# A second layer-1 bank, more of its bias on ScalarE, node copies on GpSimd and an earlier first quad, in a graph network on one core

## The chip, the cores and the metric

The kernel runs on one core of one Trainium2 chip. The metric is the device time of one execution in microseconds. Each kernel was run four times or more, on the same chip beside the kernel before; the experiments were spread over two chips, and the medians of the kernel before lie between 595.3 and 596.6 us in all rounds.

Names used below: PE is TensorE, PEld its weight loads, DVE is VectorE, ACT is ScalarE, POOL is GpSimd. A *ten* is ten chunks in a row, the period in which the kernel's plan repeats. A *turn* is a transpose by PE; its result lies in a bank until ACT or DVE has read it. For the masks of the edges, DVE's *threshold* marks the node i of each edge (`tp`), a *node copy* widens these marks from fp16 to fp32r (`i`), and a *mark product* of PE multiplies them with the *positions* (`posall`, made by POOL) to find the node j. The *bias table* is `b1t`. The *root* is the square root of the layer-0 variance (`m_sd`); `sh` holds it split into a rounded part and a rest, and making the rest is a small step of POOL. In the update network, `ysum` are the summed messages, and `uh` and `uy` the two hidden layers.

## The reference

Each of 128 graphs has 64 nodes with 128 features. For every pair (i, j) with an edge, a small network gives a message; the messages of a node are summed, and a second network updates the node.

```python
def _mlp(x, w0, b0, g0, be0, w1, b1, g1, be1, w2, b2):
    h = relu(x @ w0 + b0)
    h = layernorm(h, g0, be0)
    h = relu(h @ w1 + b1)
    h = layernorm(h, g1, be1)
    return h @ w2 + b2

messages = _mlp(concat(f_i, f_j), msg...) * adjacency[..., None]
agg      = sum(messages, axis=2)
updated  = x + _mlp(concat(x, agg), upd...)
```

All is float32. Some 13.5% of the pairs are edges (the kernel has room for 640 edges in each graph, and a slow path if that is exceeded, which does not run here: the fullest graph has 622).

## The kernel before

Edges are packed into tiles of 128. A chunk is four tiles and fills one of the kernel's banks (128x512 f32 in the trace); there are 160 chunks. Five chunks are a *quad* of graphs and share one table of statistics. The normalisation of layer 0 is folded into layer 1: with a weight matrix whose columns are centred, the layer-1 sum is `h @ w1c + sd * b1b`, where `sd` is a number for each edge, the root of the layer-0 variance. So the "bias" of layer 1 is different for each edge. It can be made in two ways: by a matmul (a table `b1t` against the turned roots `sdT`), or by ACT, which writes `b1b` scaled by `sd` into the bank ahead of the products, four instructions of 128 columns for a chunk. The second is called a *seed*.

```python
ps_k, ps_h, ps_t, ps_z, ps_y = ...           # one bank each
ps_a = ...tile_pool(name="ps_a", bufs=2, space=PSUM)   # turns
ps_u = ...                                   # update layers

def node_rows(p):                            # node marks of a pair of graphs, fp16 -> fp32r
    IR[p] = tpp.tile([P, CAP], F32R, name="i32", bufs=2)
    nc.scalar.copy(IR[p], TP[p])             # then a DMA puts it into the tile s

def layer0(n):                               # two matmuls a piece into hps, then
    ...
    nc.scalar.activation(H[n], ps, AF.Relu, bias=b0c)

def stats0(n):                               # PE turns h into the bank hT, DVE takes statistics
    ...
def seed(n):
    q, c = divmod(n, QC)
    Z[n] = zbank().rearrange("p (t c) -> p t c", t=CH)
    for t in range(CH):
        nc.scalar.activation(Z[n][:, t, :], W["b1b"], AF.Copy, scale=SR[q][:, k:k + 1])

def layer1(n):
    if n in Z:
        ps = Z.pop(n)                        # seeded
    else:
        ps = (hbank if n >= NCHK - L1 and n % 2 else zbank)()
        nc.tensor.matmul(ps, lhsT=SD[q], rhs=W["b1t"][...], start=True, stop=False, ...)
    for t in range(CH):
        nc.tensor.matmul(ps[:, t, :], lhsT=h[:, t * P:(t + 1) * P], rhs=W["w1c"], ...)
    nc.scalar.activation(Y[n], ps, AF.Relu)

for n in range(1, NCHK - L1 - 1):            # NCHK = 160, L1 = 8, CPB = 10
    if n % CPB in (0, 1, 6, 9):
        at(n + L1 - 1, "b", seed, n)
...
for n in range(last + 1):                    # the plan; every engine keeps this order
    run(n, "a"); run(n, "m")                 # "a": ACT's copies out of banks
    layer1(n - L1)
    run(n, "b")
    layer0(n)
    stats0(n - 1)
    run(n, "k")
    stats1(n - L1)
    for k in ("x", "x1", "x2", "e0", "e1", "e"):
        run(n, k)                            # "x": PE's turns and update layers
```

(cut: the making of the edge masks, the update network, the slow path, and the launch)

Eight PSUM banks hold all this: mk, hps, hT, z, ys, two for turns, one for the update layers. That an engine keeps one order shows in the traces: from 180 to 480 us the sequence of ACT's instructions repeats without an exception with every ten, 67 of them.

## Time and profile before

| | before |
|---|---|
| time, median of all runs beside the changed kernel | 595.59 us (594.19 to 598.19) |
| first layer-1 ReLU begins | 40.1 us |
| next 30 chunks | 100.3 us |
| a ten in the middle (chunks 30 to 140) | 33.88 us |
| chunks 140 to 150 | 33.2 us |
| from there to the end | 47.5 us |

The start of the ReLU that ACT makes of each layer-1 bank is a clean mark, once a chunk; the distances between the marks tell where time goes. The lines of the page and of the windows view that matter are shown in the prediction. In a line of groups, the first pair of numbers is busy time and the mean of one, and what follows is the idle time ahead of them with its releaser. PE's busy time is made of modelled ends of matmuls; this turns out to matter (300 ns between two starts where 28 ns is the shortest, below).

### The profile page before, as it was taken

What the parts mean: (1) busy time and instruction counts of PE and PEld (TensorE: products, weight loads), DVE (VectorE), ACT (ScalarE), POOL (GpSimd) and SP (SyncE); (2) the same over time, 40 slices, a digit from 0 to 9 for tenths busy, and PEclk for the clock granted to TensorE, in tenths of its full rate; (3) what the DMA queues carried; (4) which work ended last, traced back from release to release, by engine and by line L of the source; (5) the groups of instructions that cost most, each with busy time, mean ns of one, the idle gap of its engine ahead of it and who ended that gap; (6) DMA issues with size and microseconds to landing.
All of it is one profiled execution on the core that took longest, in us unless ns stands there. A gap on an engine that the chain in (4) does not pass through costs nothing. (4 is left out here: it accounts for less than half of the span.)

```text
span 593.9 us, 15761 instructions
## 1 busy us (share of the span) xinstructions
PE 565.6 (95%) x5333; PEld 521.2 (88%) x5333; DVE 480.6 (81%) x1944; ACT 479.3 (81%) x1087; POOL 296.5 (50%) x840
## 2 busy tenths in 40 slices
PE   7778899999999999999999999999999999999894
PEld 4667789899999999999999999999999999999883
DVE  4568778697988979797987979798897979788576
ACT  5677878888888888888898888888898888887434
POOL 2443435454655546365654545365654636446352
PEclk7599999999999999999999999999999999999999
DMA  4354544566454544645355445545554385531201
GB/s 98 90 120 99 134 104 109 96 121 126 114 124 109 127 106 102 147 114 131 85 140 122 98 116 120 131 114 133 97 127 110 93 143 112 107 96 37 47 19 40
DMA packets 90769, 63.22 MB, mean 106 GB/s; under 512 B 57398, under 2 KB 74812, under 8 KB 90684
## 3 DMA queue, kind: packets, MB, share of 16 engines
q1 hardware_dynamic: 90396, 62.03, 46.7%
q8 instruction: 44, 0.72, 0.6%
q14 instruction: 41, 0.34, 0.2%
q10 hardware_dynamic: 288, 0.13, 0.1%
HBM read 6.82 MB, written 4.19 MB: 19 GB/s over the span
## 5 line engine op out<-in xcount | busy, mean ns | idle before, releaser
L546 DVE BATCH_NORM_STATS2 st<-hT 128x6 f32<-128x128 f32 x640 | 141.3, 283 | 51.7 <-PE hT L542 51.7
L595 PE MATMUL z<-w1c,h 128*128 128x128 f32 x1248 | 168.3, 278 | 2.4 <-ACT z L581 2.3
L595 PEld LDWEIGHTS z<-w1c,h 128*128 128x128 f32 x1248 | 159.1, 191 | 12.6 <-issue 5.0
L605 DVE BATCH_NORM_STATS2 st<-y 128x6 f32<-128x128 f32 x640 | 137.7, 278 | 2.7 <-ACT y L598 1.4
L249 POOL TENSOR_TENSOR m_d<-st 128x20 f32<-128x20 f32 x62 | 17.1, 276 | 208.8 <-DVE st L546 188.8
L598 ACT ACTIVATE y<-z 128x512 f32<-128x512 f32 x156 | 93.5, 600 | 29.7 <-PE z L595 26.6
L536 ACT ACTIVATE h<-hps,b0c 128x512 f32<-128x512 f32 x160 | 109.1, 682 | 4.9 <-PE hps L533 4.9
L542 PE MATMUL hT<-ident,h 128*128 128x128 f32 x640 | 98.0, 276 | 2.1 <-DVE st L546 2.1
L661 POOL TENSOR_TENSOR w<-oh,m_q 128x320 f32<-128x320 f16 x126 | 91.3, 741 | 10.2 <-PE hT L542 5.6
L581 ACT ACTIVATE z<-b1b,m_sd 128x128 f32<-128x128 f32 x240 | 89.1, 371 | 7.3
L533 PE MATMUL hps<-s,abl 128*128 128x512 f32 (+3 forms) x256 | 92.7, 374 | 1.9 <-ACT h L536 1.1
L542 PEld LDWEIGHTS hT<-ident,h 128*128 128x128 f32 x640 | 76.8, 142 | 12.4 <-DVE st L546 1.4
L533 PE MATMUL hps<-s,abh 128*128 128x512 f32 (+3 forms) x256 | 79.0, 327 | 0.0
L674 PE MATMUL ys<-y,w 128*64 128x128 f32 x1280 | 76.9, 275 | 0.0
L674 PEld LDWEIGHTS ys<-y,w 128*64 128x64 f32 x1280 | 69.2, 137 | 7.0 <-issue 6.6
L515 DVE TENSOR_TENSOR j<-mk,cmpt 128x320 fp32r<-128x320 f32 x124 | 58.8, 474 | 0.5 <-PE mk L507 0.5
L479 ACT ACTIVATE d<-slot,mid 128x640 f16<-128x640 f16 x64 | 53.7, 840 | 0.0
L533 PEld LDWEIGHTS hps<-s,abl 128*128 128x128 f32 x256 | 49.8, 194 | 4.0 <-ACT h L536 2.1
L533 PEld LDWEIGHTS hps<-s,abh 128*128 128x128 f32 x256 | 49.9, 195 | 0.0
L464 ACT CAST abh<-mu 128x512 fp32r<-128x512 f32 (+1 forms) x33 | 18.9, 573 | 36.9 <-PE mu L452 36.9
L592 PE MATMUL z<-b1t,sdT 80*128 80x512 f32 x96 | 47.2, 491 | 0.6 <-ACT y L598 0.2
L491 ACT CAST i<-tp 128x640 fp32r<-128x640 f16 x62 | 44.8, 722 | 2.2 <-DVE tp L485 2.2
(218 smaller groups left out, 1005.5 us busy)
## 6 DMA issues: line engine op xcount, KB each, us to landing
s<-i SPq DMA_DIRECT2D x124, 160.0 KB, 2.7
s<-j SPq DMA_DIRECT2D x124, 160.0 KB, 2.7
xn<-in_x_dram SPq DMA_DIRECT2D x15, 256.0 KB, 3.7
out_dram<-uo SPq DMA_DIRECT2D x15, 256.0 KB, 2.4
an<-in_adj_dram SPq DMA_DIRECT2D x16, 128.0 KB, 2.6
oh<-tp SPq DMA_TRANSPOSE x64, 2.7
xn<-in_x_dram SPq DMA_DIRECT2D x2, 128.0 KB
out_dram<-uo SPq DMA_DIRECT2D x2, 128.0 KB, 2.3
```

Of the source, the lines that this page charges most:

```text
L479: nc.scalar.activation(D[p], slot, AF.Abs, bias=blocks[b]["mid"][:, q:q + 1], scale=-1.0)
L515: nc.vector.tensor_tensor(JR[p][:, c], MK.pop((p, k))[:, 0:HC], cmpt[:, c], op=ALU.is_equal)
L533: nc.tensor.matmul(ps[:, c:c + w], lhsT=ab[:, g % 4, :], rhs=s, start=(k == 0), stop=(k == 1))
L536: nc.scalar.activation(H[n], ps, AF.Relu, bias=b0c)
L542: nc.tensor.transpose(ps[:, t, :], H[n][:, t * P:(t + 1) * P], ident)
L546: nc.vector.bn_stats(ST0[q][:, CH * c + t, :], ps[:, t, :])
L581: nc.scalar.activation(Z[n][:, t, :], W["b1b"], AF.Copy, scale=SR[q][:, k:k + 1])
L595: nc.tensor.matmul(ps[:, t, :], lhsT=h[:, t * P:(t + 1) * P], rhs=W["w1c"], start=False, stop=True, skip_group_check=True)
L598: nc.scalar.activation(Y[n], ps, AF.Relu)
L605: nc.vector.bn_stats(ST1[q][:, CH * c + t, :], Y[n][:, t, :])
L661: (nc.vector if p == NP - 2 else nc.gpsimd).tensor_tensor(WT[p][:, :, g, :], OH[p][:, :, g * N:(g + 1) * N], Q[q][:, k:k + TG].unsqueeze(2 ...
L674: nc.tensor.matmul(YS[b][g * N:(g + 1) * N, k, :], lhsT=w[:, t, g, :], rhs=y, start=(t == 0), stop=(t == TG - 1))
```

## The change

The intent: PE is full, so take bias matmuls from it by seeding seven chunks of ten, not four. ACT then needs room: the node copies go to GpSimd. The seeds need time: layer 1 gets two banks by parity, so that a seed is written two chunks ahead; its bank is taken from the turns, whose plan is spread out. And at the start the first quad's layer-0 chunks are made before the masks of later pairs.

```diff
-        ps_z = ...tile_pool(name="ps_z", bufs=1, space=PSUM)
+        ps_z = [...tile_pool(name=f"ps_z{k}", bufs=1, space=PSUM) for k in range(2)]
-        ps_a = ...tile_pool(name="ps_a", bufs=2, space=PSUM)
+        ps_a = ...tile_pool(name="ps_a", bufs=1, space=PSUM)
...
-            nc.scalar.copy(IR[p], TP[p])
+            nc.gpsimd.tensor_copy(IR[p], TP[p])
...
+        def z_of(n):
+            if n not in Z:
+                Z[n] = zbank(n % 2).rearrange("p (t c) -> p t c", t=CH)
+            return Z[n]
...
-        for n in range(1, NCHK - L1 - 1):
-            if n % CPB in (0, 1, 6, 9):
-                at(n + L1 - 1, "b", seed, n)
+        for n in range(2, NCHK - L1):
+            if n % CPB in (0, 1, 2, 4, 6, 7, 9):
+                at(n + L1 - 2, "x", seed, n)
...
+        LEAD = 3
-        STEADY = (1, 2, 3, 3, 4, 7, 8, 6, 8, 9, 12, 13, 11, 14, 15)
+        STEADY = (1, 1, 2, 3, 4, 7, 8, 6, 8, 9, 12, 13, 11, 14, 15)
...
-            n = q * QC + QC
+            n = q * QC + QC if q else LEAD
...
-            if 1 < n < NCHK:
-                layer0(n)
-            if 1 <= n - 1 < NCHK - 1:
-                stats0(n - 1)
+            if n + LEAD < QC or QC <= n < NCHK:
+                layer0(n if n >= QC else n + LEAD)
+            if n + 1 < QC or QC <= n - 1 < NCHK - 1:
+                stats0(n - 1 if n > QC else n + 1)
```

(cut: the order of the first masks before the loop, the banks of the last update units, and the places of the count and of the first turn of features)

More of the change, by code (lines that the diff above doesn't have):

```diff
@@ L302, in edge_path @@
         ps_t = es.enter_context(tc.tile_pool(name="ps_t", bufs=1, space=PSUM))
-        ps_z = es.enter_context(tc.tile_pool(name="ps_z", bufs=1, space=PSUM))
+        ps_z = [es.enter_context(tc.tile_pool(name=f"ps_z{k}", bufs=1, space=PSUM)) for k in range(2)]
         ps_y = es.enter_context(tc.tile_pool(name="ps_y", bufs=1, space=PSUM))
-        ps_a = es.enter_context(tc.tile_pool(name="ps_a", bufs=2, space=PSUM))
+        ps_a = es.enter_context(tc.tile_pool(name="ps_a", bufs=1, space=PSUM))
         ps_u = es.enter_context(tc.tile_pool(name="ps_u", bufs=1, space=PSUM))
@@ L317, in hbank, with tbank, zbank @@
             return ps_h.tile([P, CH * P], F32, name="hps")
-        def zbank():
-            return ps_z.tile([P, CH, C], F32, name="z").rearrange("p t c -> p (t c)")
+        def tbank():
+            return ps_t.tile([P, CH, P], F32, name="hT").rearrange("p t c -> p (t c)")
+        def zbank(k):
+            return ps_z[k].tile([P, CH * C], F32, name=f"z{k}")
         plan = {}
@@ L430, in odd_weights, with turn_x @@
                                     axis=AX.X, op=ALU.max, apply_absolute_value=True)
-        def turn_x(b, q0=0, q1=PB):
+        def turn_x(b, q0=0, q1=PB, bank=abank):
             blk = blocks[b]
-            ps = blk["x_ps"] = abank()
+            ps = blk["x_ps"] = bank()
             for q in range(q0, q1):
@@ L572, in root_out @@
             SD[q] = t
+        SEEDED = set()
+        def z_of(n):
+            if n not in Z:
+                Z[n] = zbank(n % 2).rearrange("p (t c) -> p t c", t=CH)
+            return Z[n]
         def seed(n):
             q, c = divmod(n, QC)
-            Z[n] = zbank().rearrange("p (t c) -> p t c", t=CH)
+            z_of(n)
+            SEEDED.add(n)
             for t in range(CH):
@@ L585, in layer1 @@
             q, c = divmod(n, QC)
+            ps = z_of(n)
+            del Z[n]
             h = H.pop(n)
-            if n in Z:
-                ps = Z.pop(n)
-            else:
-                ps = (hbank if n >= NCHK - L1 and n % 2 else zbank)()
-                ps = ps.rearrange("p (t c) -> p t c", t=CH)
+            if n not in SEEDED:
                 nc.tensor.matmul(ps, lhsT=SD[q], rhs=W["b1t"][:, CH * c:CH * c + CH, :],
@@ L681, in edge_path, with __init__ @@
         class Unit:
-            def __init__(self, b, k0, n, eng, bank):
-                self.b, self.k0, self.n, self.eng, self.bank = b, k0, n, eng, bank
+            def __init__(self, b, k0, n, eng, bank, turns=abank):
+                self.b, self.k0, self.n, self.eng, self.bank, self.turns = b, k0, n, eng, bank, turns
                 self.s = slice(k0 * P, (k0 + n) * P)
@@ L716, in turn @@
         def turn(u, src):
-            u.ps = abank()
+            u.ps = u.turns()
             for q in range(u.n):
@@ L794, in edge_path @@
             if b > 0:
-                r = max(o - 13, 1)
+                r = max(o - 12, 1)
                 at(max(o - 14, 0), "m", rank, b)
@@ L819, in edge_path @@
             else:
-                units = [(Unit(b, 2, 2, nc.vector, zbank), NCHK + L1 + 1, LAST[3], 1, 1),
-                         (Unit(b, 0, 2, nc.gpsimd, hbank), NCHK + L1 - 1, LAST[2], 3, 3)]
+                units = [(Unit(b, 2, 2, nc.vector, lambda: zbank(1), tbank), NCHK + L1 + 1, LAST[3], 1, 1),
+                         (Unit(b, 0, 2, nc.gpsimd, lambda: zbank(0), hbank), NCHK + L1 - 1, LAST[2], 3, 3)]
             for u, n, t, m0_at, xo_at in units:
@@ L850, in edge_path @@
             if p > 1:
-                at(max(n - 7, p - 2), "a", distance, p)
-                at(max(n - 6, p - 2), "m", make_tp, p)
-                at(max(n - 5, 1), "a", node_rows, p)
-                at(max(n - 4, 1), "a", stack, p, 0, IR)
+                if p > 2:
+                    at(max(n - 7, p - 2), "a", distance, p)
+                    at(max(n - 6, p - 2), "m", make_tp, p)
+                at(n - 5, "a", node_rows, p)
+                at(n - 4, "a", stack, p, 0, IR)
                 for k in range(2):
@@ L867, in edge_path @@
         for q in range(NQ):
-            n = q * QC + QC
+            n = q * QC + QC if q else LEAD
             last = q == NQ - 1
+            end = q * QC + QC + L1
             at(n, "e0", var0_of, q)
@@ L873, in edge_path @@
             at(n + 2, "x" if last else "a", root_out, q)
-            at(n + L1 - last, "e1", var1_step, q)
+            at(end - last, "e1", var1_step, q)
             wait = 0 if last else 1 if q == NQ - 2 else 2
-            at(n + L1 + wait, "a", root1_of, q)
-            at(n + L1 + wait, "m", inverse_of, q)
-        for n in range(1, NCHK - L1 - 1):
-            if n % CPB in (0, 1, 6, 9):
-                at(n + L1 - 1, "b", seed, n)
+            at(end + wait, "a", root1_of, q)
+            at(end + wait, "m", inverse_of, q)
+        for n in range(2, NCHK - L1):
+            if n % CPB in (0, 1, 2, 4, 6, 7, 9):
+                at(n + L1 - 2, "x", seed, n)
         warm = ubank()
@@ L895, in edge_path @@
         count_out(0)
-        turn_x(0, 0, 2)
+        turn_x(0, 0, 2, tbank)
         turn_x_out(0, 0, 2)
@@ L910, in marks_here, with rows_here @@
             marks(p, 0)
-            marks(p, 1, zbank)
+            marks(p, 1, lambda: zbank(p % 2))
+        def rows_here(p, g):
+            nc.scalar.copy(S[p][0:N, g, :], TP[p][g * N:(g + 1) * N])
         def compare_here(p, g):
             s = slice(g * N, (g + 1) * N)
-            nc.scalar.copy(S[p][0:N, g, :], TP[p][s])
             for k in range(2):
@@ L919, in compare_here @@
                                         op=ALU.is_equal)
+            if g:
+                MK.pop((p, 0)), MK.pop((p, 1))
         marks_here(0)
         rows(0, 0, 2, 4)
+        rows_here(0, 0)
+        rows_here(0, 1)
         compare_here(0, 0)
@@ L927, in edge_path @@
         compare_here(0, 1)
-        MK.pop((0, 0)), MK.pop((0, 1))
         make_tp(1)
+        distance(2)
+        marks_here(1)
         layer0(1)
         rows_hi(0, 0, 2, 4)
-        marks_here(1)
+        rows_here(1, 0)
+        rows_here(1, 1)
         compare_here(1, 0)
         rows_lo(0, 0, 2, 4)
+        layer0(2)
+        make_tp(2)
+        compare_here(1, 1)
+        nc.vector.memset(ones_row, 1.0)
         stats0(0)
-        compare_here(1, 1)
-        MK.pop((1, 0)), MK.pop((1, 1))
-        nc.vector.memset(ones_row, 1.0)
         at(0, "x", turn_x, 0, 2, PB)
```

## The prediction

> **What bounds the kernel now.** The graphs are worked off as 160 chunks of four edge tiles. In iteration n TensorE (PE) does layer 1 of chunk n-8 (bias and product into the bank z), layer 0 of chunk n (bank hps), the turns of chunk n-1 (bank hT), and then smaller work. ScalarE (ACT) empties z and hps with ReLUs, VectorE (DVE) takes the statistics, and every engine keeps program order. I read the page first, its busy shares and its slices:
>
> ```profile
> PE 565.6 (95%) x5333; PEld 521.2 (88%) x5333; DVE 480.6 (81%) x1944; ACT 479.3 (81%) x1087; POOL 296.5 (50%) x840
> ...
> PE   7778899999999999999999999999999999999894
> ...
> PEclk7599999999999999999999999999999999999999
> ```
>
> PE is filled from about the sixth slice (75 us) on; before that it is not, and its clock is low in the first two slices. The windows view, 100 us at a time, gives the middle:
>
> ```profile
> 200.00:300.00 100.00, 99.92 (x979) 93.62 (x978) 85.36 (x348) 87.41 (x199) 53.78 (x153) 1.00 0.50 117
> 300.00:400.00 100.00, 99.91 (x980) 93.71 (x979) 85.64 (x349) 87.24 (x198) 54.61 (x156) 1.00 0.49 117
> 400.00:500.00 100.00, 99.91 (x981) 93.84 (x980) 85.58 (x349) 87.21 (x199) 54.61 (x156) 1.00 0.54 115
> ```
>
> The columns after the length are PE, weight loads, DVE, ACT, POOL (GpSimd). PE is busy 99.9 of 100 us at full clock. As ends of matmuls are modelled, I checked with starts: the ReLUs of layer 1 begin 33.9 us apart from one ten of chunks to the next, and the distances from each matmul's start to the next one's add up to the same with no hole in them. So in the middle PE alone sets the pace, and a microsecond counts there only if PE's work shrinks. The groups by line name the parts that the change touches:
>
> ```profile
> L592 PE MATMUL z<-b1t,sdT 80*128 80x512 f32 x96 | 47.2, 491 | 0.6 <-ACT y L598 0.2
> ...
> L581 ACT ACTIVATE z<-b1b,m_sd 128x128 f32<-128x128 f32 x240 | 89.1, 371 | 7.3
> ...
> L491 ACT CAST i<-tp 128x640 fp32r<-128x640 f16 x62 | 44.8, 722 | 2.2 <-DVE tp L485 2.2
> ```
>
> L592 is the bias of layer 1 as a matmul (100 in the program); L581 is the same bias written by ACT, four instructions a chunk, for 60 of 160 chunks; L491 is the node copy, 62 times. Last, the waits of PE:
>
> ```profile
> PE ma L566 <- POOL sh L561: 4.4, 4, 2.0
> PE mk L507 <- DVE tp L485: 4.4, 2, 3.2
> PE z L595 <- ACT z L581: 2.3, 4, 0.9
> ```
>
> These few (total, times, longest) all lie before 110 us. That is the start, where PE is not yet the bound.
>
> [...] the threshold L485, 0.37 us in the median, took 1.23 us when it began at 29.18 us together with a POOL product of 1.04 us; no other after 10 us is long.
>
> **The change, part by part.**
>
> *Bias matmuls.* Counting the conditions, seeds rise from 60 chunks to 105 (seven of ten, chunks 2 to 151), so bias matmuls fall from 100 to 55: 45 fewer. The page's 491 ns is not their price, as neighbours overlap. By starts in the middle, L592 begins 28 ns after the matmul before it where that is a turn of the root, and the product begins 336 ns after L592; without L592 the product begins 109 ns after such a turn. Net 28 + 336 - 109 = 255 ns; where a mark product precedes, 28 + 336 - 136 = 228. I take 250 ns. 45 x 0.25 = 11.3 us, 0.75 us of each ten chunks, nearly all on the path: PE's ten chunks go from 33.9 to about 33.1 us.
>
> *ACT.* ACT's records overlap too, so I use starts: a seed of four takes 4 x 0.38 = 1.52 us, a copy 0.615. Ten chunks gain three seeds (+4.6) and lose four copies (-2.5): +2.1. All ACT instructions of ten chunks add up to 28.8 us this way (85% of 33.9), afterwards 30.9 (93% of 33.1). Still under PE, but no longer far.
>
> *Two banks.* The seed was written between the ReLU of chunk n-1 and PE's need of z for chunk n, with one bank. Now it is written two iterations ahead, into the bank that chunk n-2 has left, after the ReLU that empties hps. PE's waits for seeds (2.3 us and as much again of weight loads, partly the same time) should go: 2 us, early.
>
> *One bank less for turns.* ps_a falls from two buffers to one. The order of the program shows how they made room: before, features and counts, and the turns of ysum and uy, fell into the same iteration; after, every user has its own, and ACT empties each at the head of the next. I charge 0 to 1 us.
>
> *Node copies on POOL.* No copy is in the trace there. POOL's iota of 640 elements took 0.66 us, its 512-wide residual sum with two inputs 1.28 us; I estimate 0.8 us, so 62 x 0.8 = 50 us, and POOL goes from 54% to some 65% in the middle. A copy has an iteration or more before its DMA is due, so this lies beside PE's work. What it can cost is DVE waits of the kind seen at 29 us.
>
> *Start.* The first ReLU of layer 1 begins at 40.1 us. From 9 to 40 us PE is busy 22.6 us by the windows view and idle 8.4, of it 3.2 for the threshold that DVE reaches late and 2.0 for the roots (L566). With three layer-0 chunks ahead and the first statistics done two iterations earlier, these two waits are attacked; the total work up to there is the same, and it runs partly at low clock. I estimate 2 to 3 us. *End:* other banks, same order: 0.
>
> Sum: -11.3 (bias matmuls) -2 (seed waits) -2.5 (start) +2 to 3 (new waits) = about -13.
>
> **Rivals.**
>
> *ACT becomes the bound in places.* For: iterations are unequal. Over four light ones (layer 1 of chunks 81 to 84) PE has 1.9 + 2.5 + 3.4 + 2.0 = 9.7 us afterwards and ACT 2.3 + 3.3 + 2.3 + 3.3 = 11.2, a lag of 1.5 us; before it was 10.2 against 9.4, with a lag of 1.0 at most after the first. PE needs hps emptied each iteration. Against: a seed now stands behind the ReLU that PE waits for, so that much lag can be borne, and an iteration of 5.4 us on PE follows in which ACT catches up. If 0.5 us of each ten chunks is lost, 7 us go and the result is near 589 us.
>
> *POOL blocks or delays.* [...] Against: a copy starts as its threshold ends[...]; only in the start do POOL queues look crowded (the bias table, five products of 1.04 us).
>
> *The start gives more.* If PE closes most of its gaps between 9 and 110 us (8.4 us, and 5.9 after 40 us), the total could reach 576. Against: ACT and DVE are 75 to 85% busy in the slices after 45 us.
>
> **Range and chances.** I say 582.5 us. 576 needs the start to give far more, 590 needs ACT or POOL to eat over half of the gain. The 2% line is at 595.86 x 0.98 = 583.9, within my error; so faster 0.58, same 0.40, slower 0.02.
>
> **What would show it right or wrong.** In the profile after: L592's successor with 55 instances (some records may be missing); PE still at 99% or more in the middle, and ten chunks 33.1 us apart. If instead PE falls to 97 or 98% there, with waits for ACT h or y ahead of hps or z, the first rival holds. ACT should stand at about 94 to 95% in the middle by the page's count, POOL at 63 to 68%, a copy at 0.6 to 1.0 us[...]. PE's seed waits should be gone, and the first ReLU of layer 1 should begin at 37 to 38 us. The prediction fails if the price of 250 ns is wrong, if the period hangs on something besides PE, or if the start moves by over 5 us.

## The result

| | before | after |
|---|---|---|
| time, median | 595.59 us (594.19 to 598.19) | 588.81 us (588.71 to 589.01) |
| first layer-1 ReLU | 40.1 us | 40.7 us |
| next 30 chunks | 100.3 us | 96.1 us |
| a ten in the middle | 33.88 us | 33.47 us |
| chunks 140 to 150 | 33.2 us | 34.0 us |
| from there to the end | 47.5 us | 48.0 us |

The ratio is 0.988, with a 95% interval of 0.985 to 0.992: faster, by less than 2%. Ratios here and below are the mean time of one kernel's fast runs over that of the other's fast runs of the same rounds, so they are not quite the ratio of the medians. The stretches are of the profiled run, spans 593.9 and 587.0 us. Before rounding they add up: +0.5 at the start, -4.1 in the next 30 chunks, -4.5 in the middle (eleven tens of 0.41), +0.8 and +0.4 at the end, -6.9 in all. A ten is a steady measure: the four profiles with the seeds of the changed kernel and the same middle (the changed kernel, e3, e7, e11) have 33.47 to 33.48 us. The first ReLU is not: the six profiles with the start of the changed kernel have it at 40.7 to 42.3 us, so that 0.5 us there says nothing.

The page of the changed kernel, the busy shares, the row of PE's clock, and the two groups of seeds and node copies:

```profile
PE 553.7 (94%) x5288; PEld 512.9 (87%) x5288; DVE 480.7 (82%) x1944; ACT 492.4 (84%) x1205; POOL 340.9 (58%) x902
...
PEclk9979999999999999999999999999999999999998
...
L594 ACT ACTIVATE z<-b1b,m_sd 128x128 f32<-128x128 f32 x420 | 156.1, 372 | 10.2
...
L494 POOL CAST i<-tp 128x640 fp32r<-128x640 f16 x62 | 44.5, 718 | 77.2 <-DVE tp L488 61.4
```

There are 420 seed instructions where there were 240, and a copy takes 0.718 us on POOL, as long as on ACT (0.722). The windows view, 100 us in the middle, in the order PE, PEld, DVE, ACT, POOL, then PE's clock, the DMA share and GB/s:

```profile
200.00:300.00 100.00, 98.78 (x980) 93.12 (x979) 86.71 (x353) 91.18 (x225) 62.91 (x169) 1.00 0.54 119
```

PE fell from 99.9 to 98.8 busy, at a kernel that should have left PE full. The waits of PE name the places, over the whole span first and then for weight loads in the middle (173 to 507 us):

```profile
PEld ma L569 <- POOL sh L564: 15.0, 17, 6.8
...
PE ma L569 <- POOL sh L564: 9.6, 4, 6.5
PEld mu L744 <- ACT uhT L735: 7.4, 13, 0.6
...
PE ma L730 <- ACT ysumT L735: 1.9, 1, 1.9
```

```profile
PEld mu L744 <- ACT uhT L735: 5.7, 10, 0.6
...
PEld ma L569 <- POOL sh L564: 3.3, 10, 0.3
```

Two waits come once in every ten: for the turned `uh` (0.6 us on the weight load) and for the root `sh` (0.3 us). Two come once in the run: 6.5 us at the start and 1.9 us near the end. The seed waits of before are gone.

Here is one ten's place of the two waits, instructions in order of time, ACT first and then PE of the same stretch:

```profile
311.70 0.69 ACT L539 ACTIVATE h<-hps,b0c 128x512 f32<-128x512 f32 x1
312.27 0.41 ACT L767 ACTIVATE usdb<-bu1b,um_sd 128x128 f32<-128x128 f32 x1
312.56 1.59 ACT L594 ACTIVATE z<-b1b,m_sd 128x128 f32<-128x128 f32 x4
314.09 0.58 ACT L735 COPY uhT<-ma 128x512 f32<-128x512 f32 x1
314.56 0.60 ACT L609 ACTIVATE y<-z 128x512 f32<-128x512 f32 x1
315.05 0.31 ACT L259 ACTIVATE m_sd<-m,eps_c 128x20 f32<-128x20 f32 x1
315.39 0.22 ACT L563 CAST sh<-m_sd 128x40 fp32r<-128x40 f32 x1
```

```profile
311.57 0.60 PE L730 MATMUL ma<-ident,uh 128*128 128x128 f32 x4
...
314.15 0.30 PE L510 MATMUL mk<-tp,posall 128*128 128x320 f16 x1
314.72 1.16 PE L744 MATMUL mu<-u1c,uhT 128*128 128x128 f32 x8 [0.27 <-ACT uhT L735]
316.01 0.31 PE L569 MATMUL ma<-ident,sh 128*80 128x128 f32 x1
```

PE has turned `uh` by 312.2 us. ACT could copy it out then, but a seed of 1.59 us stands ahead in its order, and the copy begins at 314.09. PE's update layer starts at 314.72; after a mark product it would have started 0.14 us after 314.15. The delay is 0.43 us. Everything of ACT after it is late by as much, the root too, and PE waits another 0.30 us for `sh` (its normal distance is 0.11 us, here 0.41). If PE's distances from start to start are added up pair by pair, the same pairs take 0.86 us of a ten more here than in e2 below: these 0.43 and 0.30, and another 0.12 between the products of this update layer (the first two are 0.21 us apart, not 0.11). The seed in question is that of chunks with n mod 10 = 4.

And the start, POOL's instructions in order of time:

```profile
25.99 0.22 POOL L253 TENSOR_TENSOR m<-m_d,m_s 128x20 f32<-128x20 f32 x1
26.17 1.51 POOL L397 TENSOR_TENSOR posall<-pos,an 64x256 f16<-64x256 f32 x2
27.75 0.17 POOL L625 MEMSET own<- 128x80 f32 x1
...
30.20 0.60 POOL L642 TENSOR_SCALAR b1mix<-b1hi,part 128x128 f32<-128x128 f32 x1
30.88 0.45 POOL L643 TENSOR_TENSOR b1mix<-b1mix,b1lo 128x128 f32<-128x128 f32 x1
31.29 0.27 POOL L564 TENSOR_TENSOR sh<-m_sd,sh 128x40 fp32r<-128x40 f32 x1
```

The variance of the first quad is ready at 26.2 us (before: 34.6). ACT has made the root by 26.8. But POOL's last step on it, 0.27 us long, stands behind the positions of the next block and the whole bias table, and comes at 31.3. PE waits for it from 25 us. With that wait goes a loss of clock: in the row of the page above, PE's clock is low in the third slice; by the trace it is at half (0.50) from 27.0 us on for 10.24 us.

### The profile page after: what moved, and what is told of

Its sections match the earlier page's. It is cut to its first block, busy times and chain, and to the rows that moved or that the text cites. A ratio compares the mean times of both kernels' runs of the same rounds, so it can differ in the third digit from the quotient of the medians.

```text
span 587.0 us, 15781 instructions
## 1 busy us (share of the span) xinstructions
PE 553.7 (94%) x5288; PEld 512.9 (87%) x5288; DVE 480.7 (82%) x1944; ACT 492.4 (84%) x1205; POOL 340.9 (58%) x902
## 5 line engine op out<-in xcount | busy, mean ns | idle before, releaser
L606 PE MATMUL z<-w1c,h 128*128 128x128 f32 x1280 | 172.3, 278 | 0.0
L594 ACT ACTIVATE z<-b1b,m_sd 128x128 f32<-128x128 f32 x420 | 156.1, 372 | 10.2
L536 PE MATMUL hps<-s,abl 128*128 128x512 f32 (+3 forms) x256 | 93.9, 379 | 1.8 <-ACT h L539 1.1
L494 POOL CAST i<-tp 128x640 fp32r<-128x640 f16 x62 | 44.5, 718 | 77.2 <-DVE tp L488 61.4
L249 POOL TENSOR_TENSOR m_d<-st 128x20 f32<-128x20 f32 x62 | 15.9, 257 | 93.0 <-DVE st L549 80.8
L473 DVE TENSOR_TENSOR abl<-mu,abh 128x512 fp32r<-128x512 f32 (+1 forms) x33 | 22.3, 675 | 33.8 <-ACT abh L467 33.4
```

The costliest lines, as they stand in the source:

```text
L536: nc.tensor.matmul(ps[:, c:c + w], lhsT=ab[:, g % 4, :], rhs=s, start=(k == 0), stop=(k == 1))
```

## The experiments

Every experiment is an edit of the changed kernel, unless it says otherwise, and gave a correct result. A ten means chunks 30 to 140 of the profiled run.

### One seed moved, or dropped (e1, e2)

```diff
-            if n % CPB in (0, 1, 2, 4, 6, 7, 9):
+            if n % CPB in (0, 1, 2, 5, 6, 7, 9):      # e1
+            if n % CPB in (0, 1, 2, 6, 7, 9):         # e2
```

> As the changed kernel, but the seed of chunks 4 of each ten is given to chunks 5 instead, so still 105 seeds and 55 bias matmuls. It is then written after ScalarE has copied the turned uh and made the root, not just before. Theory 1 (place: that one seed stands ahead of uhT and of the root in ScalarE's order, and PE waits 0.43 us and 0.30 us for them in each ten): the two waits go, ten chunks fall from 33.47 to 32.7 to 32.9 us, the total to 577 to 581 us, PE in the middle back to 99.5% or more. Theory 2 (load: ScalarE has simply too much work, 93% by starts): the waits move to another place, ten chunks stay at 33.3 to 33.5 us and the total at 587 to 589 us.

> As the changed kernel without the seed of chunks 4 of each ten: 90 seeds, 70 bias matmuls. Theory 1 (place): the waits of 0.73 us go, a bias matmul of 0.25 us comes back, so ten chunks take 32.9 to 33.1 us and the total is 581 to 584 us. Theory 2 (load): part of the waits stays, 33.2 to 33.5 us, 585 to 589 us. If the waits do not come from this seed at all, ten chunks take 33.7 us and the total is 592 us.

Measured: e1 583.84 us (ratio to before 0.978), a ten 32.97 us; e2 583.16 us (0.978), a ten 32.83 us. Windows view, e1 and then e2:

```profile
200.00:300.00 100.00, 99.71 (x993) 94.78 (x992) 87.87 (x359) 92.74 (x229) 64.51 (x174) 1.00 0.56 120
```

```profile
200.00:300.00 100.00, 100.00 (x1000) 95.65 (x999) 88.12 (x362) 89.55 (x218) 65.22 (x173) 1.00 0.57 123
```

In both, the waits for `uhT` and `sh` are gone. So it was that seed at that place. e2 is in the range of theory 1, with a ten just under it. With fifteen bias matmuls *more*, e2 is 5.6 us faster than the changed kernel. e1 missed its range (577 to 581): moved, the seed still costs PE 0.3 us in each ten, now in a wait for the layer-0 ReLU:

```profile
PEld hps L536 <- ACT h L539: 2.9, 10, 0.3
```

A ten of 32.97 us lies between the ranges of both theories (32.7 to 32.9, 33.3 to 33.5). The place explains most of the loss; for the rest a wait that moves fits the second theory, but a third place was not tried. At either of the two places tried, a seventh seed costs more than it saves.

### The seeds of before, all else changed (e6)

```diff
-            if n % CPB in (0, 1, 2, 4, 6, 7, 9):
+            if n % CPB in (0, 1, 6, 9):
```

> The changed kernel with the seeds of the kernel before: chunks 0, 1, 6 and 9 of ten, 60 seeds and 100 bias matmuls, all else as changed. Theory 1 (each seed is worth 0.25 us of PE, and the one of chunks 4 costs 0.73 us of waits): ten chunks take 33.47 + 0.75 - 0.73 = 33.5 us, the total is 587 to 590 us, so the three more seeds of ten brought nothing together. Theory 2 (the seeds brought the gain, the waits come from the single bank for turns or from GpSimd's copies): waits stay, ten chunks take 34.2 us, the total is 599 us.

Measured: 589.77 us, a ten 33.29 us, PE at 100.00 in the middle. The time is theory 1's, a ten is shorter than its 33.5 us. (The total hides this: in this profile PE's clock was at half for 20.5 us at the start and for 3.4 us in chunks 140 to 150, which took 35.7 us.) With e2 it gives the price of a bias matmul without any wait in the way: two more seeds of ten, (33.29 - 32.83) / 2 = 0.23 us each. And it shows a gain that no bias matmul explains: with 60 seeds in both, a ten went from 33.88 to 33.29.

### Where those 0.59 us come from (e8, e9)

e8 is the kernel *before* with the node copies on GpSimd. e9 is e6 with the copies back on ScalarE.

```diff
-            nc.scalar.copy(IR[p], TP[p])          # e8, on before; e9 the other way round
+            nc.gpsimd.tensor_copy(IR[p], TP[p])
```

> The kernel before with one part of the change alone: node copies on GpSimd. One bank for layer 1, 60 seeds. In the trace of before, PE's bias matmul begins 30 to 50 ns after the ReLU of the chunk before has left the one bank, twice in each ten chunks, and twice that costs 0.03 and 0.2 us; ScalarE's copies stand ahead of those ReLUs. Theory A (the copies make those ReLUs late): ten chunks fall from 33.88 to 33.5 to 33.65 us and the total by 4 to 6 us. Theory B (one bank is the cause by itself; ScalarE is not needed sooner): 33.8 to 33.9 us, total within 1.5 us of before.

> The changed kernel with the seeds of before (60) and with the node copies back on ScalarE: of the parts in the middle only the two banks and the spread turns are left. The same with copies on GpSimd took 33.29 us for ten chunks. Theory A (the copies on GpSimd bring the 0.6 us by which that is under the 33.88 of before): 33.7 to 33.9 us, total 594 us or more. Theory B (two banks bring it): 33.25 to 33.4 us, total 588 to 591 us.

| a ten, 60 seeds in all four | copies on ACT | copies on POOL |
|---|---|---|
| one z bank, two for turns | 33.88 (before) | 33.58 (e8) |
| two z banks, one for turns, plan and seeds shifted | 34.07 (e9) | 33.29 (e6) |

e8 took 590.64 us (0.993), e9 599.51 us (1.007, slower than before). Both bear out theory A, though a ten of e9 is longer than its 33.7 to 33.9. The place can be read in the trace of the kernel before, ACT and then PE in order of time:

```profile
316.07 0.73 ACT L491 CAST i<-tp 128x640 fp32r<-128x640 f16 x1
316.69 0.84 ACT L479 ACTIVATE d<-slot,mid 128x640 f16<-128x640 f16 x1
317.42 0.31 ACT L273 ACTIVATE m_sq<-m_v,eps_c 128x20 f32<-128x20 f32 x1
317.62 0.59 ACT L598 ACTIVATE y<-z 128x512 f32<-128x512 f32 x1
```

```profile
317.63 0.60 PE L719 MATMUL ma<-ident,uh 128*128 128x128 f32 x4
318.26 0.49 PE L592 MATMUL z<-b1t,sdT 80*128 80x512 f32 x1
```

The ReLU ends at 318.21 us and the bias matmul into the same bank begins at 318.26. The last of the four turns before it began at about 317.96 and is given 0.275 us, so the page counts nearly no idle time; but where nothing holds it, a bias matmul follows a turn after 28 ns, and here it came after 0.30 us. A copy (0.62 us to the next start) stood ahead of that ReLU in ACT's order. In e8 this distance is 28 ns again, and that alone is 0.27 of the 0.30 us. With two banks and the copies on ACT (e9) the ReLU holds nobody up, but the single turn bank does: PE waits for ACT's copy of the turned root.

```profile
PEld ma L439 <- ACT sdT L574: 5.2, 9, 0.6
```

So the parts need each other: the second z bank, bought with a turn bank and a shifted plan, costs 0.19 us of a ten by itself, and brings 0.29 once ACT is freed. Half of the 0.29 can be placed: two bias matmuls in each ten that follow a turn of h begin 60 and 140 ns after it in e8 and 28 ns after it in e6, 0.14 us together.

### The start (e3, e7)

```diff
-        at(3, "e", bias_table)
+        at(5, "e", bias_table)                    # e3
-            at(4 + c, "e", bias_part, c)
+            at(6 + c // 2, "e", bias_part, c)
```

e7 takes the lead of the first quad back (the conditions of the last hunk of the change, the iteration of its root, the first masks and the order before the loop) and leaves all else.

> As the changed kernel, but the bias table that GpSimd builds is put two iterations later (its five parts too), so that GpSimd's part of the first quad's root no longer stands behind it, nor VectorE's small reduction. Theory 1 (queue: PE's wait of 6.5 us for that root at 25 to 31.6 us is GpSimd's order alone): the wait falls under 2 us, the first layer-1 ReLU begins at 36 to 37.5 instead of 40.7 us, total 584 to 586 us. Theory 2 (the start hangs on other work, such as the transfers of the second pair's masks or VectorE): the first ReLU stays at 39.5 to 41 us and the total at 588 to 589 us.

> The changed kernel with the order of the start undone: layer-0 chunks and statistics of the first quad at the iterations of before, the roots of that quad made after iteration 5. Middle unchanged, 33.47 us. Theory 1 (the lead brought the statistics forward by 8 us but the gain was lost to the root's wait behind the bias table on GpSimd): the first layer-1 ReLU begins at 39.5 to 41 us as in both kernels, total 588 to 590 us, and the wait for the root is about 2 us. Rival (the lead does bring something, hidden by a slower start elsewhere): the first ReLU at 43 us or later, total 591 to 593 us.

Measured: e3 584.70 us (0.981), first ReLU at 35.2 us, PE's wait for the root 3.0 us where it was 6.5. e7 588.17 us (0.988), first ReLU at 39.8 us, wait 2.2 us. Both times are theory 1's; the first ReLU of e3 is earlier than the 36 to 37.5 expected, and its wait longer. The profile of e3 is of the fastest of its four executions (583.3 to 585.9). The lead brought nothing that can be measured as it stood in the change, and what it should have brought lay behind the bias table.

The rest of the wait in e3, 3.0 us and not under 2, is the two positions (1.5 us) and the chain of small steps. Not all of the gain is the wait: it is 3.5 us shorter and the first ReLU 5.5 us earlier. In all six profiles with the wait of 6.5 us (the changed kernel, e1, e2, e6, e9, e11) PE's clock is at half for 10.24 us in or just after it; after the shorter waits of e3, e10 and e13 for 3.4 to 6.8 us. What the clock's share is was not tested; earlier stretches of half clock (20.5 us before and in e7, 6.8 us in e3, none in the changed kernel) differ as well.

### The end (e11)

Where the last blocks (eight graphs each) begin, one block's turn of `uy` and the next block's turn of `ysum` fall into the same iteration. The change shifted the plan of the steady blocks by one for this reason, but not the first row of the plan for the last ones.

```diff
-        LAST = ((1, 2, 3, 3, 4, 5, ...
+        LAST = ((1, 1, 2, 3, 4, 5, ...
```

> The changed kernel with one mend alone: in the last blocks the turn of ysum comes one iteration earlier, so that it and the turn of uy don't share the one turn bank in an iteration. In the trace PE waits 1.9 us there for ScalarE, and in some runs (not in the profiled one of the changed kernel) the clock falls to half for 3.4 us after it. Theory 1 (the halved turn buffers cost these 1.9 us, and up to 1.6 us of clock in some executions): 585 to 587 us. Theory 2 (the last blocks are bound by their chain of updates): 588 to 589 us.

Measured: 586.94 us (0.985), and the stretch of chunks 140 to 150 falls from 34.0 to 31.9 us. Theory 1. There is a second cost, which not every profile shows. In the runs with this wait (the changed kernel, e1, e2, e3, e6, e7, e9), five of seven profiles show PE's clock at half for 3.4 us just after it; in the six profiles without it (before, e8, e10 to e13), none does. Windows view of e7, three stretches:

```profile
523.00:526.40 3.40, 3.40 (x35) 3.09 (x32) 2.49 (x11) 2.54 (x6) 0.00 (x0) 1.00 0.62 145
526.40:529.80 3.40, 1.48 (x12) 1.11 (x11) 2.68 (x14) 3.06 (x7) 1.24 (x6) 1.00 0.00 0
529.80:533.20 3.40, 3.40 (x16) 3.22 (x17) 0.28 (x1) 0.61 (x2) 0.55 (x1) 0.51 0.02 5
```

PE was busy 1.48 of 3.4 us in the second, and has clock 0.51 in the third. In the profiles of the changed kernel and of e3 the clock held. The stretches of half clock in these traces last 3.41 us or whole multiples of it (20.48 us before, 10.24 us in the changed kernel; the last one, cut off by the end, excepted), and their starts within a trace lie whole multiples apart (583.7 us before, 171 times 3.413; 556.4 us in the changed kernel, 163 times). If each trace is divided into steps of 3.413 us from these starts, the step with the wait has PE busy 1.50 to 1.51 us in the five profiles, 1.55 in the changed kernel, and 2.17 in e3, where the wait falls into two steps. What decides the clock was not shown: no limit of busy time comes out of these traces, as in the start 1.72 us was followed by half clock in e3, and 1.71 was not in e2.

### All together (e10, e12, e13)

e10 is the changed kernel with e2, e3 and e11. e12 is e10 with the lead taken back. e13 is e10 with the first quad's small step on the root on VectorE.

```diff
-            eng_of(q).tensor_tensor(SH[q][:, 2:4, :], sdb, ...)
+            (eng_of(q) if q else nc.vector).tensor_tensor(SH[q][:, 2:4, :], sdb, ...)   # e13
```

> The changed kernel with three mends together: no seed for chunks 4 of ten (15 seeds fewer), the bias table two iterations later, and in the last blocks the turn of ysum one iteration earlier, so that it does not share the single turn bank with the turn of uy, for which PE waits 1.9 us at chunk 147. If the three causes are independent, the gains of the first two runs (5.6 and 4.1 us under 588.8) and about 2 us add up: 576 to 578.5 us. If the later start or end is bound by something they share (the last chunks' update chain), 579 to 583 us.

> The three mends together, with the lead of the first quad's chunks undone. With the lead it took 575.0 us. Theory 1 (the lead pays once the bias table no longer stands ahead of the root on GpSimd): 577 to 580 us, first layer-1 ReLU at 39 to 41 us. Theory 2 (the late table alone gives the gain at the start, the lead gives nothing): 574 to 576 us, first ReLU at 36 to 38 us.

> The three mends together, and the small difference of the first quad's root on VectorE instead of GpSimd. PE still waits 3.0 us for that root at 25 to 28 us, of it 1.5 us while GpSimd writes two positions first. Theory 1 (GpSimd's order is what is left of that wait): the wait falls to 2.2 us or less, first ReLU 0.7 us or more earlier, total 573 to 574.5 us. Theory 2 (it is hidden by later work): 574.5 to 575.5 us.

| | time, us | to before | first ReLU | a ten | 140 to 150 |
|---|---|---|---|---|---|
| before | 595.59 | 1 | 40.1 | 33.88 | 33.2 |
| changed | 588.81 | 0.988 | 40.7 | 33.47 | 34.0 |
| e10 | 575.01 | 0.966 | 37.3 | 32.83 | 31.2 |
| e12 | 581.54 | 0.974 | 43.4 | 32.83 | 31.2 |
| e13 | 574.70 | 0.963 | 37.6 | 32.83 | 31.2 |

e10 beats both kernels, by 3.4% and (0.966 / 0.988) 2.3%. The three mends add up, and a little more than expected: 5.6 + 4.1 + 1.9 = 11.6 us by the single runs, 13.8 together. The stretches of the profiles say where: from the changed kernel to e10 it is -3.4 us at the start, -0.2, -7.1 in the middle and -2.8 in chunks 140 to 150. e2 alone also gained 7.0 us in the middle, but in its profile the start was 1.6 us longer and chunks 140 to 150 were 1.0 us longer than in the changed kernel, the latter with 3.4 us of half clock.

e12 fits neither of its theories. Without the lead, the late table stands ahead of the root again, which is then made later; PE's wait for it is 4.6 us there. So the lead and the late table only work as a pair: 575.0 with both, 581.5 with the late table alone, which the two runs show (on different chips, and with first ReLUs of 37.3 and 43.4 us); e7 has shown that the lead alone, with the early table, is worth nothing that can be measured.

e13 is within the spread of e10 (574.1 to 575.8 against 573.5 to 575.6); the wait went from 3.0 to 2.7 us only, not to 2.2. The total is theory 2's, but within that spread it decides nothing. Its trace shows one reason: the step took 0.75 us on VectorE, where it takes 0.27 on GpSimd, just when GpSimd wrote the positions; the threshold ahead of it took 0.72 us (0.73 in e10 at the same place), where the median is 0.37.

## Why the prediction was right or wrong

The time lay in the range and the class was the less likely one of two. The size was off: 13 us forecast, 6.8 measured. That the time still lay in the range is partly luck: without the 0.59 us of a ten that nobody forecast (below), a ten would have been 34.06 us, longer than before. Step by step:

- **PE bounds the middle: right, but "with no hole in it" was wrong.** The distances from start to start were added up, and a sum contains the holes; they were not compared with what the same pair of instructions takes unhindered. That would have shown 0.27 us of a ten at the bias matmul of one chunk, which waited for the ReLU on the single bank, and 0.14 us at two others. Closing these and smaller ones is worth 0.59 us of a ten (e6), which the prediction did not foresee. Nor do all the waits that it lists lie before 110 us: 0.5 of the 2.3 us for seeds fall at 545 us. It was cautious about parts of the change that turned out to carry it.
- **The price of a bias matmul, 0.25 us: right.** It is 0.23 us (e2 against e6).
- **"Still under PE, but no longer far" and "that much lag can be borne": this step failed.** The argument looked at the layer-0 ReLU alone, which stands ahead of the seed. It did not ask what stands *behind* the seed in ACT's order and is needed by PE in the next iteration: the turned `uh` and the root. The first rival named the mechanism, ACT's lag over the four light iterations, and even its outcome (0.5 us of a ten, 589 us), and was then argued away. In a ten, the two waits are 0.73 us (0.43 and 0.30), where the sum had 2 to 3 us for the whole run. The third added seed made a ten longer by 0.64 us (32.83 to 33.47); that is 0.87 us lost less the 0.23 us it saved.
- **The sum of a ten:** forecast -0.75; measured -0.41, from -0.59 (two banks, copies and spread turns together), -0.46 (two seeds) and +0.64 (the third).
- **The early tens: the sum right, the parts not.** Forecast -2.25 for bias matmuls and -2 for seed waits, measured -4.1. But e6, with the seeds of before, already has 97.1 us there, -3.1: that much came from the banks, the place of the seeds and the copies. The added seeds brought -1.0.
- **The start, -2.5: failed, measured +0.5** (less than such profiles differ by). The statistics did come eight us earlier, but the wait "attacked" grew from 2.0 to 6.5 us. The prediction saw that POOL's queue was crowded at the start and did not follow it to the root, which passes through it.
- **"After, every user has its own": wrong in one place.** It holds in the steady blocks, where I read the order, and not in the last ones. 1.9 us, where 0 to 1 was charged.
- **Copies on POOL: right.** 0.718 us against an estimate of 0.8; POOL at 62.9% in the middle, just under the 63 to 68 given. In the middle the thresholds of DVE did not become longer: they stay at 0.369 us in the median (before 0.370), and the only long ones lie in the start (up to 1.09 us, at 34.7 us, while POOL made a product of the bias table). Why those are long no run tested. ACT stands at 91.2%, under the 94 to 95 given; a ten of 33.1 us would have made it 92.2% (an estimate: 30.5 us of ACT), so about one point is the longer ten, and the rest was not looked into.

## What to carry to other kernels

When work moves to an engine that others wait for, read that engine's order and ask of each added piece what comes *after* it and who needs that next; a share of 93% says little about it. A busy share of 99.9% whose ends are modelled can hide waits: compare each distance from start to start with the shortest one of the same pair (here 300 ns against 28 ns). The busy share of weight loads did tell the cases apart here: 93.6 to 93.8% in the kernel before, 95.4 to 95.7% in e2, e6 and e10. When a bank or a queue place is given up, check the plan of the first and the last blocks as well as of the steady ones, and try one step less of a change (six seeds, not seven) before keeping it.
